# Band attention on folded score tiles: softmax sums and weighted values as 64-row matmuls in two places of a step, and band groups normalized in other steps

## The chip, the cores and the metric

One core of a Trainium2 chip runs the whole program. The metric is device time in microseconds (us). A core has five engines that run their own instruction streams and wait for each other by semaphores: TensorE (PE; its weight loads are shown apart as PEld), VectorE (DVE), ScalarE (ACT), GpSimd (POOL) and SyncE (SP), which issues most DMA transfers. The on-chip memory SBUF has 128 partitions; TensorE writes into PSUM, eight banks of 128 partitions x 512 float32. All data are float32.

## The reference

`x` has the shape (2, 256, 128, 128): two batches, 256 times, 128 bands, 128 channels. One layer:

```
cm = causal_mask(256)             # time j <= time i
bm = band_mask(128, 16)           # |band i - band j| <= 16
x = x + MHA(LN(x), over the 256 times of each band, cm)     # 4 heads of 32
x = x + MHA(LN(x), over the 128 bands of each time, bm)     # 4 heads of 32
x = x + GELU(LN(x) @ w1.T + b1) @ w2.T + b2                 # 128 -> 512 -> 128
MHA: q, k, v = split(x @ wi.T + bi); softmax(q k^T / sqrt(32) + mask) v; @ wo.T + bo
```

## The kernel before

A group is four tiles of 128 tokens (`NT = 4`), 512 columns, and is an object whose methods issue the work of one stage. 128 groups of class `OverTime` come first. Then 16 cycles follow, each of 8 `OverBands` groups (here called k0 to k7; 32 times of one batch, `RUN = 32`) and 8 `FeedForward` groups (f0 to f7) over the same 32 times, whose tokens stay in SBUF as `res` between the two. A cycle takes about 106 us.

`BoundedPath.run` is one loop over n with an order written out by hand. Step n does the scores of group n, the softmax sums and weighted values of n-1 (`weigh`), the output product of n-2, queries, keys and values of n+1, and the layer norm of n+3 (`normalize`, `turn`). The helper `InOrder` passes each instruction on and pins it to program order on its engine, so every operation carries the helper's line, L907 in the profile (L968 in the changed kernel); rows are told apart by tile names.

What a band group does:

- `scores`: for each tile, half of keys and head, a 32x64 matmul `kT` x `qT`. Tokens are bands, so 64 keys see only the 80 queries from 16 below to 16 above: 64 keys by 80 queries. There are four banks `sp`, one for each head; the result lies at its place in a tile of 128 keys x 128 queries, so that a bank has 512 columns, of which 48 in each half tile are not written by these matmuls.
- `first_function`: DVE adds the mask `band` to the scores of the last head (head 3; `by_vector = 1` is the number of such heads), and ACT takes exp of all four heads into `pf` (512 columns each).
- `first_mask`: POOL zeroes what lies outside the band in the other three heads, by two `affine_select` each.
- `weigh`: `sums` of the weights come from matmuls with a matrix of ones (`rp`), the weighted values from `v` (`op`), with all 128 keys on the rows and 32 output rows a head: 4 matmuls of 512 columns, and 16 of 128.
- `invert` (ACT: `ln`, then `r` = exp(-ln)) and `divide` (DVE: one refinement of the reciprocal in `rp`, giving `u`, and `oT` = `op` x `u`), then `output` (`wn`, `oT` into `yp`) and `finish` (DVE: add to x).
- `queries_keys`, `values`: `wf` and `xnT` into `qp`, `kp`, `vp`, which ACT copies out (`qT`, `kT`, `v`).
- `statistics`, `root` (DVE, POOL: `stats`, `mv`, `rstd`), `normalize` (DVE: four `xh`, and a transpose `z` of 32x32 blocks), `turn` and `fetch` (SP: DMAs through DRAM tiles `turned` that finish the transpose as `xnT`).

A feed group does `hidden` (`xnT`, `w1f` into `hp`, two and two banks), GELU by ACT into `hT`, and `weigh` (`w2T_sb`, `hT` into `zp`), which DVE adds to `res`.

The eight PSUM banks go round in order (`turn_of_bank`), two places being held back for `yp` and `qp` of the next groups. float32 matmuls are carried out in two passes: each matmul of the program is two MATMUL and two LDWEIGHTS in the profile. A matmul with 32 output columns of weights uses one of four column strips of the array, and the four strips (in `scores`, eight tiles of 32x64) run beside each other.

Of the kernel before, what the change touches and what calls it, by code (L numbers as in the profile page):

```python
# [33 lines left out]
HALF = P // 2  # L34
LARGE = 1e20
# [334 lines left out]
class Group:  # L370
# [7 lines left out]
    def __init__(self, path, src, dst, before=None, store=None):  # L378
        self.path, self.src, self.dst = path, src, dst
        self.before, self.store = before, store  # L380

# [179 lines left out]
class Attention(Group):  # L561
# [9 lines left out]
    def queries_keys(self):  # L571
        path = self.path
        wf = path.k.wf[self.which]
        self.qp = path.bank([P, NT * P], "qp", self.place.get("qp", path.held.pop("qp", None)))
        product(path, self.qp, wf[:, 0:P], self.xnT)

        self.kp = path.bank([P, NT * P], "kp", self.place.get("kp"))
        product(path, self.kp, wf[:, P : 2 * P], self.xnT)

    def take_query(self):  # L580
        path = self.path
        self.qT = path.work.tile([P, NT * P], F32, name="qT")
        path.scalar.activation(self.qT, self.qp, AF.Identity, bias=path.k.bq[self.which], scale=1.0)

    def take_key(self):
        path = self.path
        self.kT = path.work.tile([P, NT * P], F32, name="kT")
        path.scalar.copy(self.kT, self.kp)

    def values(self):  # L590
        path = self.path
        wv = path.k.wf[self.which][:, 2 * P : 3 * P]
        self.vp = path.bank([P, NT, P], "vp", self.place.get("vp"))
        for i in range(NT):
            product(path, self.vp[:, i], self.xnT[:, i * P : (i + 1) * P], wv, turn=2 if i in self.swapped else 0)

    def take_values(self):
        path = self.path
        self.v = path.work.tile([P, NT, P], F32, name="v", bufs=4)
        path.scalar.copy(self.v, self.vp)  # L600

# [13 lines left out]
    def divide(self):  # L615

        path, vector = self.path, self.path.vector
        if self.r0 is None:
            self.oT = path.work.tile([P, NT * P], F32, name="oT", bufs=2)
            u = path.work.tile([P, NT * P], F32, name="u", bufs=2)  # L620
            vector.tensor_tensor(by_rows(u), by_tile(self.op), by_tile(self.r), ALU.mult)
            vector.tensor_scalar(self.oT, u, -1.0, None, ALU.mult)
            return
# [4 lines left out]
        vector.tensor_tensor(by_rows(self.oT), by_tile(self.op), by_tile(u), ALU.mult)  # L628

    def output(self):  # L630
        path = self.path
        self.yp = path.bank([P, NT, P], "yp", self.place.get("yp", path.held.pop("yp", None)))
        for i in range(NT):
            product(path, self.yp[:, i], self.oT[:, i * P : (i + 1) * P], path.k.wn[self.which])

    def finish(self):
        self.path.vector.tensor_tensor(self.dst(), self.yp, self.dst(), ALU.add)
        if self.store is not None:
            self.store()
# [13 lines left out]
class OverTime(Attention):  # L653
# [7 lines left out]
    def values(self):  # L661
        path = self.path
        wv = path.k.wf[self.which][:, 2 * P : 3 * P]
        self.vp = [path.bank([P, 2, P], "vp", self.place.get(f"vp{s}")) for s in range(2)]
# [5 lines left out]
    def take_values(self):  # L670
        path = self.path
        self.v = path.work.tile([P, NT, P], F32, name="v", bufs=4)
        for s in range(2):
            path.scalar.copy(self.v[:, 2 * s : 2 * s + 2], self.vp[s])

    def first_tiles(self):
# [3 lines left out]
        self.s0 = {h: path.bank([P, 2, 2 * P], "sp", path.banks[f"a{h}"]) for h in range(H)}  # L680

    def second_tiles(self):
# [3 lines left out]
        self.s1 = {h: path.bank([P, 2, P], "sp", path.banks[f"b{h}"]) for h in range(H)}  # L686
# [15 lines left out]
    def first_weights(self, heads):  # L702
        for h in heads:
            self.path.scalar.activation(self.p0[:, :, h], self.s0[h], AF.Exp)

    def second_weights(self, heads):
        for h in heads:
            self.path.scalar.activation(self.p1[:, :, h, 0], self.s1[h], AF.Exp)

# [17 lines left out]
    def weigh(self):  # L727
        path, v = self.path, self.v
        rp = path.bank([P, 2, 2, P], "rp", self.place.get("rp"))
# [4 lines left out]
        op = path.bank([P, 2, 2 * P], "op", self.place.get("op"))  # L734
# [33 lines left out]
class OverBands(Attention):  # L768
# [3 lines left out]
    follow = ("yp",)  # L772
    by_vector = 1

    def scores(self, heads):
        path = self.path
        self.sp = {h: path.bank([P, NT * P], "sp") for h in heads}
        for i in range(NT):
            for e in range(2):
                keys = slice(e * HALF, (e + 1) * HALF)  # L780
                a = i * P + e * (HALF - BAND)
                q = slice(a, a + HALF + BAND)
                for h in heads:
                    r = rows_of(h)
                    path.tensor.matmul(
                        self.sp[h][keys, q], self.kT[r, i * P + e * HALF : i * P + (e + 1) * HALF], self.qT[r, q],
                        start=True, stop=True,
                    )

    def first_function(self):  # L790
        path = self.path
        for h in range(H - self.by_vector, H):
            sp = self.sp[h].rearrange("p (i q) -> p i q", i=NT)
            path.vector.scalar_tensor_tensor(
                sp, sp, LIMIT, path.band.unsqueeze(1).to_broadcast([P, NT, P]), ALU.min, ALU.add
            )
        for h in range(H):
            path.scalar.activation(self.p[:, h].rearrange("p i q -> p (i q)"), self.sp[h], AF.Exp)

    def first_mask(self):  # L800
        path = self.path
        for h in range(H - self.by_vector):
            blk = self.p[:, h]
            for s in (1, -1):
                path.gpsimd.affine_select(
                    out=blk, in_=blk, compare_op=ALU.is_ge, fill=path.zero, base=BAND,
                    pattern=[[0, NT], [-s, P]], channel_multiplier=s,
                )

    def first_half(self):  # L810
        self.p = self.path.work.tile([P, H, NT, P], F32, name="pf", tag="p", bufs=3)
        self.scores(range(H))

    def weigh(self):
        path = self.path

        path.held = {name: path.turn_of_bank() for name in self.follow}
        self.rp = path.bank([P, NT * P], "rp")
        for h in range(H):
            path.tensor.matmul(  # L820
                self.rp[rows_of(h), :], path.k.ones[:, 0:D], self.p[:, h].rearrange("p i q -> p (i q)"),
                start=True, stop=True,
            )
        self.op = path.bank([P, NT * P], "op")
        for i in range(NT):
            c = slice(i * P, (i + 1) * P)
            for h in range(H):
                r = rows_of(h)
                path.tensor.matmul(self.op[r, c], self.v[:, i, r], self.p[:, h, i, :], start=True, stop=True)


class FeedForward(Group):
# [8 lines left out]
    def hidden(self, js):  # L841
        path = self.path
        for j in js:
            self.hp[j] = path.bank([P, NT * P], "hp")
            product(path, self.hp[j], path.k.w1f[:, j * P : (j + 1) * P], self.xnT)

    def gelus(self, js):
        path = self.path
        for j in js:
# [3 lines left out]
            )  # L853

# [14 lines left out]
    def weigh(self):  # L869
        path, NI = self.path, self.path.k.NI  # L870
        if self.last:
            zp = [path.bank([P, P], "zp") for i in range(NT)]
        else:
            self.zp = path.bank([P, NT, P], "zp")
# [11 lines left out]
    def divide(self):  # L886
# [5 lines left out]
        else:  # L892
            self.path.vector.tensor_tensor(self.dst(), self.zp, self.dst(), ALU.add)
        self.store()
# [17 lines left out]
class BoundedPath:  # L912
    def __init__(self, ctx, tc, k):
# [6 lines left out]
        self.next_bank = 0  # L920
        self.inputs = 0
        self.held = {}
# [5 lines left out]
        self.dram = ctx.enter_context(tc.tile_pool(name="turns", bufs=3, space=DRAM))  # L928
# [6 lines left out]
        self.band = once.tile([P, P], F32, name="band")  # L935
        tc.nc.gpsimd.memset(self.band, 0.0)
        for s in (1, -1):
            tc.nc.gpsimd.affine_select(
                out=self.band, in_=self.band, compare_op=ALU.is_ge, fill=-1e30, base=BAND,
                pattern=[[-s, P]], channel_multiplier=s,  # L940
            )

    def turn_of_bank(self):
        i, self.next_bank = self.next_bank, (self.next_bank + 1) % 8
        return i

    def bank(self, shape, name, i=None):

        flat = self.ps[self.turn_of_bank() if i is None else i][:, 0 : math.prod(shape[1:])]
# [4 lines left out]
        return flat.rearrange(f"p ({' '.join(names)}) -> p {' '.join(names)}", **sizes)  # L954

# [218 lines left out]
    def verdict(self):  # L1174

        vector, C = self.vector, P
        tp = self.bank([P, 6], "tp")
# [97 lines left out]
    def run(self, x, out):  # L1275
# [15 lines left out]
        for i in range(len(groups) - 2):  # L1291
            if at(i, OverBands) and at(i + 1, OverBands):
                groups[i].follow = ("yp", "qp")

# [18 lines left out]
        for n in range(len(groups) + 2):  # L1313
# [70 lines left out]
            do_at(n + 3, (OverBands, FeedForward), "normalize", "turn")  # L1384
# [128 lines left out]
```

## Time and profile before

| | |
|---|---|
| three runs | 2632.67, 2633.2, 2638.77 us (median 2633.2) |
| the profiled execution, first to last instruction (its span, the only time shown of it) | 2631.9 us |
| its instructions | 156,460; the granted TensorE clock 1.000 |
| `OverTime` part | about the first 926 us |
| one cycle of band and feed groups | about 106.2 us, 16 times |
| one band step, from scores to scores | 6.23 us |
| one feed step | 6.92 to 6.93 us |
| busy shares | PE 99%, DVE 81%, POOL 74%, ACT 70% |

In the timeline rows a number pair is the start and the length in us; the length of a run of pipelined matmuls reaches past the start of the next, so the start of one row to the start of the next is what it costs TensorE. `[0.30 <-issue]` is idle time ahead of the row and what ended it; `issue` means that the engine waited for nothing that the profile shows. A row of windows gives the stretch, its length, then for PE, PEld, DVE, ACT and POOL the busy time and (x) the instructions, the granted clock, the DMA engines' busy share and GB/s. In the groups the columns are: busy us, mean ns of one | idle us ahead and what ended it.

### The profile page before, as it was taken

The page shows a single profiled execution, that of the slowest core. Times are in us where ns is not written, and L with a number is a line of the kernel's source. Part 1 is how long each engine was busy: PE and PEld are TensorE (multiplying, and loading weights), DVE is VectorE, ACT ScalarE, POOL GpSimd, SP SyncE. Part 2 cuts the span into 40 slices and gives each one's busy share as a digit, 9 for nine tenths or more (in the row PEclk, how much of TensorE's full clock was granted, in tenths as well). Part 3 has the DMA queues.
Part 4 walks back from the last instruction along what each step waited for, and adds up shares of the span by engine and source line. Part 5 has one row for each costly group of instructions (what it writes and reads, how often), then busy time and mean ns, then how long its engine had stood idle before and what let it go on. Part 6 is the DMA issues. An engine that isn't in the chain of part 4 may idle for free.

```text
span 2631.9 us, 156460 instructions
## 1 busy us (share of the span) xinstructions
PE 2617.8 (99%) x68688; PEld 1837.4 (70%) x68688; DVE 2140.8 (81%) x6410; ACT 1838.8 (70%) x3543; POOL 1958.6 (74%) x2311
## 2 busy tenths in 40 slices
PE   9999999999999999999999999999999999999999
PEld 6666666666766767666777776667676677777776
DVE  8888888888888887977878779788797797887974
ACT  7989988999899875564655746647557466475573
POOL 7999999999999987666667666665776666757762
PEclk9999999999999999999999999999999999999999
DMA  6656555565565454445454544554454445554543
GB/s 155 167 149 158 149 149 149 155 155 149 149 158 149 122 127 119 115 123 127 118 124 124 123 122 117 126 128 120 122 126 120 120 119 131 123 120 123 123 104 88
DMA packets 469797, 344.97 MB, mean 131 GB/s; under 512 B 43120, under 2 KB 404464, under 8 KB 469104
## 3 DMA queue, kind: packets, MB, share of 16 engines
q1 hardware_dynamic: 468408, 334.41, 50.5%
q8 instruction: 540, 8.85, 1.5%
q14 instruction: 153, 1.25, 0.2%
q10 hardware_dynamic: 696, 0.46, 0.1%
HBM read 167.98 MB, written 166.72 MB: 127 GB/s over the span
## 4 chain that ended last, share of the span: by engine, by line
PE 99%; DVE 0%; issue 0%; DMA 0%; ACT 0%; ACTq 0%; DVEq 0%
PE bank L907 99%; DMA x<-in_x 0%; DVE xh L907 0%; DVE bank L907 0%; DVE res L907 0%; DVE stats L907 0%; DVE oT L907 0%; DVE u L907 0%; DVE xnT L907 0%; ACTq L907 0%; ACT p L907 0%; DVE vy L907 0%; ACT lnv L907 0%; DVE mv L907 0%; ACT root L907 0%
## 5 line engine op out<-in xcount | busy, mean ns | idle before, releaser
L907 ACT ACTIVATE hT<-bank,b 128x512 f32<-128x512 f32 x512 | 348.1, 688 | 524.2 <-PE bank L907 483.2
L907 POOL TENSOR_SCALAR_AFFINE_SELECT pf<-pf 128x512 f32<-128x512 f32 x768 | 477.7, 637 | 185.3 <-ACT pf L907 159.1
L907 PEld LDWEIGHTS bank<-w2T_sb,hT 128*32 128x32 f32 x16384 | 467.4, 110 | 54.8 <-issue 29.0
L907 PE MATMUL bank<-xnT,wf 128*32 128x512 f32 x4096 | 492.4, 592 | 0.5 <-DVE xnT L907 0.5
L907 PE MATMUL bank<-xnT,w1f 128*32 128x512 f32 x4096 | 486.3, 592 | 0.2 <-issue 0.2
L907 PE MATMUL bank<-w2T_sb,hT 128*32 128x128 f32 x16384 | 482.8, 273 | 1.0 <-issue 1.0
L907 ACT ACTIVATE p<-bank 128x512 f32<-128x512 f32 (+1 forms) x1024 | 430.6, 494 | 62.9 <-PE bank L907 62.9
L907 DVE TENSOR_SCALAR xh<-x,mv,rstd 128x160 f32<-128x160 f32 (+1 forms) x1012 | 394.3, 432 | 59.7 <-POOL rstd L907 49.4
L907 POOL TENSOR_SCALAR_AFFINE_SELECT p<-p 128x1024 f32<-128x1024 f32 (+2 forms) x384 | 364.5, 949 | 57.5 <-ACT p L907 49.1
L907 PEld LDWEIGHTS bank<-wf,xnT 128*32 128x32 f32 x8192 | 243.3, 110 | 144.1 <-issue 101.6
L907 POOL TENSOR_TENSOR p<-p,p 128x512 f32<-128x512 f32 x256 | 324.6, 1291 | 10.6
L907 DVE BATCH_NORM_STATS2 stats<-x 128x6 f32<-128x128 f32 x1536 | 329.0, 276 | 3.4 <-DMA x<-in_x 3.4
L907 POOL TENSOR_SCALAR rstd<-mv 128x4 f32<-128x4 f32 x251 | 57.8, 230 | 361.7 <-DVE mv L907 360.5
L907 PEld LDWEIGHTS bank<-xnT,w1f 128*32 128x32 f32 x4096 | 183.6, 110 | 171.6 <-issue 109.6
L907 PE MATMUL bank<-qT,kT 32*64 32x80 f32 (+4 forms) x16384 | 302.0, 271 | 0.1
L907 PEld LDWEIGHTS bank<-qT,kT 32*64 32x64 f32 x16384 | 260.0, 131 | 51.2 <-ACT kT L907 50.6
L907 DVE TENSOR_TENSOR res<-bank,res 128x512 f32<-128x512 f32 (+1 forms) x259 | 170.3, 658 | 153.3 <-PE bank L907 144.7
L907 ACT ACTIVATE pf<-bank 128x512 f32<-128x512 f32 x512 | 265.8, 602 | 35.5 <-PE bank L907 31.3
L907 PE MATMUL bank<-wn,oT 128*32 128x128 f32 x8192 | 283.8, 274 | 0.1
L907 DVE STREAM_TRANSPOSE z<-xh 128x512 f32<-128x512 f32 x380 | 270.3, 711 | 13.3
L907 PE MATMUL bank<-wf,xnT 128*32 128x128 f32 x8192 | 276.5, 273 | 0.0
L907 POOL TENSOR_TENSOR rstd<-rstd,mhalf 128x4 f32<-128x4 f32 x251 | 260.8, 1039 | 20.9
(100 smaller groups left out, 3820.3 us busy)
## 6 DMA issues: line engine op xcount, KB each, us to landing
turned<-z SPq DMA_DIRECT2D x1520, 64.0 KB, 2.7
xnT<-turned SPq DMA_DIRECT2D x380, 256.0 KB, 3.2
x<-res SPq DMA_DIRECT2D x256, 128.0 KB, 2.5
x<-x SPq DMA_DIRECT2D x128, 256.0 KB, 4.1
out<-res SPq DMA_DIRECT2D x252, 128.0 KB, 2.3
x<-in_x SPq DMA_DIRECT2D x124, 256.0 KB, 4.3
x<-in_x SPq DMA_DIRECT2D x4, 128.0 KB, 2.8
x<-in_x SPq DMA_DIRECT2D x6, 64.0 KB, 2.9
```

The source lines that it names most:

```text
L907: return self.tc.keep_in_program_order(emit(*args, **kwargs))
```

## The change

1. Scores are folded: the bank of a head holds `[P, NT, REACH]` with `REACH = 80`: 64 keys on the lower and 64 on the upper partitions, each with its own 80 queries. Exp, masks and `pf` have 320 columns instead of 512.
2. POOL's six `affine_select` become three multiplications with a 0/1 tile `keep`. DVE's mask is still that of head 3 (`by_vector` is now the head itself), and comes later, just ahead of `weigh(n-1)`; head 3's exp comes after `ln` and `r` of n-1 on ACT.
3. Sums and values are 64-row matmuls of 80 columns, one for each half of keys: 8 program matmuls for the sums and 32 for the values instead of 4 and 16. Both halves add into the same bank over the 32 middle queries. They are issued in two places: `weigh_first(n-1)` (sums of half 1, values of half 0) ahead of the scores of n, where the groups n-1 and n are band groups; and `weigh(n-1)` (sums of half 0, values of half 1) behind them. Its first matmul waits for `seen`, a copy by ACT of one element of what `weigh_first` wrote.
4. The banks are a free list: `give` puts a bank at its end when its reader has been issued, `take` takes the first.
5. In all cycles but the first, band groups are normalized at n-6 where the current step is a band or feed step for which that is due, instead of n-3: in a cycle, the steps k0, k1 do one band group each (the last two of the eight), k2 to k4 none, k5 to k7 the feed groups f0 to f2, and the feed steps f2 to f4 a feed and a band group each. The DRAM pool of `turned` has 8 buffers instead of 3.
6. In the first feed step f0, `output` and `finish` of k6 come between `weigh_first` and `weigh` of k7.

The core of the diff:

```diff
+REACH = HALF + BAND
 class Group:
+    def take(self, name, shape, i=None):
+        free = self.path.free
+        if i is None:
+            i = free[0]
+        if i in free:
+            free.remove(i)
+        self.taken[name] = i
+        return self.path.bank(shape, name, i)
...
 class OverBands(Attention):
-    by_vector = 1
+    by_vector = 3
+    def scores(self):
+        self.sp = {h: self.take(f"sp{h}", [P, NT, REACH]) for h in range(H)}
...
+                keys, a = slice(e * HALF, (e + 1) * HALF), i * P + e * (P - REACH)
+                    path.tensor.matmul(
+                        self.sp[h][keys, i], self.kT[r, i * P + e * HALF : i * P + (e + 1) * HALF],
+                        self.qT[r, a : a + REACH], start=True, stop=True,
+                    )
+    def first_mask(self):
+        keep = path.keep.unsqueeze(1).to_broadcast([P, NT, REACH])
+        for h in range(H):
+            if h != self.by_vector:
+                path.gpsimd.tensor_tensor(self.p[:, h], self.p[:, h], keep, ALU.mult)
...
+    def part(self):
+        seen = path.small.tile([P, 1], F32, name="seen")
+        self.seen = path.scalar.copy(seen, self.op_[:, NT - 1, 0:1])
+    def sums(self, e):
+        rows, a = slice(e * HALF, (e + 1) * HALF), e * (P - REACH)
+        for h in range(H):
+            m = self.path.tensor.matmul(
+                self.rp_[rows_of(h), :, a : a + REACH], self.path.k.ones[rows, 0:D], self.p[rows, h],
+                start=e == 1, stop=True, skip_group_check=True,
+            )
+            if e == 0 and h == 0:
+                self.behind(m)
+    def weighted(self, e):
+        rows, a = slice(e * HALF, (e + 1) * HALF), e * (P - REACH)
+        for i in range(NT):
+            for h in range(H):
+                r = rows_of(h)
+                self.path.tensor.matmul(
+                    self.op_[r, i, a : a + REACH], self.v[rows, i, r], self.p[rows, h, i],
+                    start=e == 0 and i == 0, stop=True, skip_group_check=True,
+                )
+    def weigh_first(self):
+        self.rp_ = self.take("rp", [P, NT, P])
+        self.op_ = self.take("op", [P, NT, P])
...
+        self.sums(1)
+        self.weighted(0)
+        self.part()
+    def weigh(self):
+        self.sums(0)
+        self.weighted(1)
...
-        self.dram = ctx.enter_context(tc.tile_pool(name="turns", bufs=3, space=DRAM))
+        self.dram = ctx.enter_context(tc.tile_pool(name="turns", bufs=2 * NT, space=DRAM))
...
 def run(self, x, out):
+        def turn_ahead(n):
+            for i in (n + 3, n + 6):
+                if at(i, FeedForward) and i == n + 3 or at(i, OverBands) and (i == n + 3 or n > run0[0] and i not in run0):
+                    if not hasattr(groups[i], "turned"):
+                        do(i, "normalize", "turn")
...
+            if bands[1] and bands[2]:
+                do(n - 1, "weigh_first")
             do(n, "first_half", "first_function", "first_mask")
...
-            do_at(n + 3, (OverBands, FeedForward), "normalize", "turn")
+            turn_ahead(n)
...
+            do_at(n, OverBands, "late_mask")
+            if turn:
+                do(n - 1, "weigh_first")
+                do(n - 2, "output", "finish")
             do(n - 1, "weigh")
             do(n - 1, "invert_exactly" if turn else "invert")
+            do_at(n, OverBands, "late_function")
...
-            if bands[2] or turn:
+            if bands[2]:
                 do(n - 2, "output", "finish")
```

How the order moves is shown in the seventh run of band groups, from the last two scores of group k3 on. In a row the first name is what is written, the others what is read, and the size is that of one result; `bank_108` to `bank_115` are the eight PSUM banks, `xN` at the end counts alike rows.

On TensorE before, from the end of one step's scores to the next step's:

```order
L907 MATMUL bank_114<-qT,kT 64x80
L907 MATMUL bank_115<-qT,kT 64x80
L907 MATMUL bank_110<-pf,ones 32x512 x4
L907 MATMUL bank_111<-pf,v 32x128 x16
L907 MATMUL bank_108<-wn_241,oT 32x128 x16
L907 MATMUL bank_109<-xnT,wf_238 32x512 x4
L907 MATMUL bank_112<-xnT,wf_238 32x512 x4
L907 MATMUL bank_113<-wf_238,xnT 32x128 x16
L907 MATMUL bank_114<-qT,kT 64x80
L907 MATMUL bank_115<-qT,kT 64x80
```

On TensorE after, the same stretch:

```order
L968 MATMUL bank_112<-qT,kT 64x80
L968 MATMUL bank_110<-qT,kT 64x80
L968 MATMUL bank_114<-pf,ones 32x4x80 x4
L968 MATMUL bank_113<-pf,v 32x80 x16
L968 MATMUL bank_108<-wn_253,oT 32x128 x16
L968 MATMUL bank_115<-xnT,wf_250 32x512 x4
L968 MATMUL bank_109<-xnT,wf_250 32x512 x4
L968 MATMUL bank_111<-wf_250,xnT 32x128 x16
L968 MATMUL bank_112<-pf,ones 32x4x80 x4
L968 MATMUL bank_110<-pf,v 32x80 x16
L968 MATMUL bank_108<-qT,kT 64x80
L968 MATMUL bank_114<-qT,kT 64x80
```

The sums and values of 512 and 128 columns have become 4 and 16 of 80 columns behind the scores, and as many again, of the next group, ahead of the next scores. Those scores take banks 114 and 113, which hold the sums and weighted values of the group before.

On ACT before, the same step:

```order
L907 ACTIVATE pf<-bank_112 128x512
L907 ACTIVATE pf<-bank_113 128x512
L907 ACTIVATE pf<-bank_114 128x512
L907 ACTIVATE pf<-bank_115 128x512
L907 ACTIVATE ln<-bank_110 128x512
L907 ACTIVATE r_33769<-ln 128x512
L907 ACTIVATE qT<-bank_109,bq_283 128x512
L907 COPY kT<-bank_112 128x512
L907 COPY v<-bank_113 128x512
```

On ACT after:

```order
L968 COPY seen<-bank_113 128x1
L968 ACTIVATE pf<-bank_109 128x320
L968 ACTIVATE pf<-bank_111 128x320
L968 ACTIVATE pf<-bank_112 128x320
L968 ACTIVATE ln<-bank_114 128x512
L968 ACTIVATE r_34758<-ln 128x512
L968 ACTIVATE pf<-bank_110 128x320
L968 ACTIVATE qT<-bank_115,bq_295 128x512
L968 COPY kT<-bank_109 128x512
L968 COPY v<-bank_111 128x512
```

Three exps stand ahead of `ln` instead of four, and the fourth behind `r`; the copy `seen` stands ahead of all.

On DVE before, the same step:

```order
L907 SCALAR_TENSOR_TENSOR bank_115<-bank_115,band 128x512
L907 TENSOR_SCALAR xh<-x_58,mv,rstd 128x5x32 x4
L907 STREAM_TRANSPOSE z<-xh 128x512
L907 TENSOR_TENSOR x_31475<-bank_108,x_31475 128x512
L907 TENSOR_TENSOR bank_110<-bank_110,r_33769 128x512
L907 SCALAR_TENSOR_TENSOR u<-bank_110,r_33769 128x512
L907 TENSOR_TENSOR oT<-bank_111,u 128x4x4x32
L907 BN_STATS stats<-x_31475 128x6 x4
L907 BN_AGGR mv<-stats 128x2 x4
```

On DVE after:

```order
L968 SCALAR_TENSOR_TENSOR bank_110<-bank_110,band 128x320
L968 TENSOR_TENSOR x_32316<-bank_108,x_32316 128x512
L968 TENSOR_TENSOR bank_114<-bank_114,r_34758 128x512
L968 SCALAR_TENSOR_TENSOR u<-bank_114,r_34758 128x512
L968 TENSOR_TENSOR oT<-bank_113,u 128x4x4x32
L968 BN_STATS stats<-x_32316 128x6 x4
L968 BN_AGGR mv<-stats 128x2 x4
```

`xh` and `z` are gone from this step; the release of banks 114 and 113 is the third to fifth row.

More of the change, by code (lines that the diff above doesn't have):

```diff
@@ L663, in values @@
         wv = path.k.wf[self.which][:, 2 * P : 3 * P]
-        self.vp = [path.bank([P, 2, P], "vp", self.place.get(f"vp{s}")) for s in range(2)]
+        self.vp = [self.take(f"vp{s}", [P, 2, P], self.place.get(f"vp{s}")) for s in range(2)]
         for i in range(NT):
@@ L679, in first_tiles @@
         self.p0 = path.work.tile([P, 2, H, 2 * P], F32, name="p0", tag="p", bufs=3)
-        self.s0 = {h: path.bank([P, 2, 2 * P], "sp", path.banks[f"a{h}"]) for h in range(H)}
+        self.s0 = {h: self.take(f"s0{h}", [P, 2, 2 * P], path.banks[f"a{h}"]) for h in range(H)}
     def second_tiles(self):
@@ L685, in second_tiles @@
         self.p1 = path.work.tile([P, 2, H, 2, P], F32, name="p1", tag="h", bufs=2)
-        self.s1 = {h: path.bank([P, 2, P], "sp", path.banks[f"b{h}"]) for h in range(H)}
+        self.s1 = {h: self.take(f"s1{h}", [P, 2, P], path.banks[f"b{h}"]) for h in range(H)}
     def first_scores(self, h, s, e):
@@ L800, in first_mask @@
     def first_mask(self):
         path = self.path
[L802 to L812, printed above, removed]
@@ new lines, in late_function, with behind @@
+    def late_function(self):
+        self.weights(self.by_vector)
+    def part(self):
+        path = self.path
+        seen = path.small.tile([P, 1], F32, name="seen")
+        self.seen = path.scalar.copy(seen, self.op_[:, NT - 1, 0:1])
+    def behind(self, matmul):
+        self.path.tc.add_manual_dep(
+            matmul.ins, self.seen.ins.name,
+            mybir.DependencyInfo(mybir.DependencyClass.Sync, mybir.DependencyReason.DATA),
+            reason="row tiles take turns in a bank",
+        )
```

108 lines of the change are left out of this document (56 added, 52 removed).

## The prediction

> **What bounds the kernel now.** I read the page's totals and the chain that ended last first, then TensorE's timeline over a band step, then the places where TensorE stands still.
>
> ```profile
> span 2631.9 us, 156460 instructions
> PE 2617.8 (99%) x68688; PEld 1837.4 (70%) x68688; DVE 2140.8 (81%) x6410; ACT 1838.8 (70%) x3543; POOL 1958.6 (74%) x2311
> PE 99%; DVE 0%; issue 0%; DMA 0%; ACT 0%; ACTq 0%; DVEq 0%
> q8 instruction: 540, 8.85, 1.5%
> ```
>
> TensorE is the bound: 99% of the chain. The last line is a queue that loads instructions: 540 packets of 8.85 MB, 16 KB each. TensorE executes 68,688 matmuls and as many weight loads, 137,376 in all, or 254 to a packet, so this is its code. One band step:
>
> ```profile
> 1603.52 0.40 PE L907 MATMUL bank<-wf,xnT 128*32 128x128 f32 x8
> 1603.85 0.97 PE L907 MATMUL bank<-qT,kT 32*64 32x80 f32 x64
> 1604.74 1.07 PE L907 MATMUL bank<-pf,ones 128*32 128x512 f32 x8
> 1605.63 1.06 PE L907 MATMUL bank<-pf,v 128*32 128x128 f32 x32
> 1606.50 1.06 PE L907 MATMUL bank<-wn,oT 128*32 128x128 f32 x32
> 1607.37 1.90 PE L907 MATMUL bank<-xnT,wf 128*32 128x512 f32 x16
> 1609.09 1.06 PE L907 MATMUL bank<-wf,xnT 128*32 128x128 f32 x32
> 1610.08 0.97 PE L907 MATMUL bank<-qT,kT 32*64 32x80 f32 x64
> ```
>
> From start to start: scores 0.89 (0.90 below), sums 0.89, values 0.87, output 0.87, queries and keys 1.72, v 0.99; 6.23 us in all, with no idle time. Each matmul has a weight load, so a step is 184 + 184 = 368 instructions. Where does TensorE stop?
>
> ```profile
> 1568.70 1.74 PE L907 MATMUL bank<-w2T_sb,hT 128*32 128x128 f32 x56 [0.20 <-issue]
> 1599.81 0.64 PE L907 MATMUL bank<-pf,v 128*32 128x128 f32 x16 [0.30 <-issue]
> 1568.69:1599.80 31.11, 30.81 (x896) 19.90 (x896) 25.77 (x61) 24.35 (x45) 20.09 (x34) 1.00 0.46 115
> 1565.49:1568.69 3.20, 3.02 (x138) 2.65 (x136) 2.06 (x5) 3.11 (x5) 0.56 (x1) 1.00 0.13 44
> 1778.13:1780.81 2.68, 2.68 (x134) 2.58 (x131) 1.54 (x4) 2.52 (x4) 0.00 (x0) 1.00 0.02 6
> 1353.45:1357.01 3.56, 3.14 (x144) 2.78 (x142) 2.48 (x6) 3.53 (x6) 0.94 (x2) 1.00 0.02 5
> 1357.01 0.75 PE L907 MATMUL bank<-w2T_sb,hT 128*32 128x128 f32 x20 [0.42 <-issue]
> ```
>
> The two stops of this cycle wait for nothing that the profile shows, in the middle of runs of like matmuls, and between them lie 896 + 896 = 1792 = 7 x 256 instructions: they fall on the ends of 16 KB packets. The three short windows are single packets of 256 (the counts include what was in flight at the ends): 3.20 and 3.56 us are packets that ended in a stop, 2.68 one that did not. So I read the stops as a packet that ran out before the next had landed, the next being asked for only when this one starts. A packet must then last at least a time L, seen here at 2.68 or less to 3.56; before, hardly any stretch of 256 instructions is shorter than that.
>
> **The change, part by part.**
>
> *Sums and values.* The two pieces cost 0.89 + 0.87 = 1.76 us. Each becomes halves of 80 columns: a slot (sums of one half beside values of the other) has 8 + 32 matmuls and 40 loads, 80 instructions. The sums' row gives the column rate: 2 passes of 512 in 0.89 us. In a slot each of eight tiles gets 2 x 4 x 80 = 640 columns, 0.56 us; the scores, also 640 columns in each of eight tiles with as many loads as the values have here, take 0.90. Ends 0.56 and 0.90; I take 0.72 between them, because the slot issues 80 instructions to the scores' 128 but has the same eight loads in half its tiles. A step is now scores 0.90, slot 0.72, output 0.87, queries and keys 1.72, v 0.99, slot 0.72: 5.92 instead of 6.23, with 128 + 80 + 64 + 32 + 64 + 80 = 448 instructions. In a run of eight groups: 8 x (1.76 - 1.44) = 2.56 us less. In f0 the output stands between the two slots: two more changes of tile shape, each about the 0.99 - 0.87 by which v outlasts the output product of the same size, 0.1 as an estimate. Net -2.36 us a run.
>
> *Code.* 448 instructions in 5.92 us are 256 in 3.38 on average, but unevenly. Cutting four steps (1792) into seven packets from the start of the scores, with each piece's instructions spread evenly, gives 2.27, 4.10, 4.01, 2.36, 4.44, 2.06 and 4.44 us. If long packets give nothing to short ones, the stops are the sum of what each lacks to L. At 3.20: 0.93 + 0.84 + 1.14 = 2.91 for four steps, 0.73 a step, and for the seven steps of a run with both slots 5.1 us. At 2.68 it is 1.35, 0.34 a step, 2.4 a run; at 3.56 it is 3.99, 1.0 a step, 7.0 a run. I take 3.20, the middle row. Five normalizes' DMAs leave the band steps and the window of 3.20 has DMA share 0.13, those of 2.68 and 3.56 both 0.02, so DMA load doesn't order them. The old stops, 0.20 + 0.30 in this cycle, are within the new ones: -0.5.
>
> [...]
>
> *Banks.* The next scores of heads 1 and 2 now write the banks of sums and values of the group before, so they wait for its divide. The pieces of that loop:
>
> ```profile
> 1572.96 0.97 PE L907 MATMUL bank<-qT,kT 32*64 32x80 f32 x64
> 1573.97 2.07 ACT L907 ACTIVATE pf<-bank 128x512 f32<-128x512 f32 x4 [0.29 <-PE bank L907]
> 1575.90 0.63 ACT L907 ACTIVATE ln<-bank 128x512 f32<-128x512 f32 x1
> 1576.56 0.63 ACT L907 ACTIVATE r<-ln 128x512 f32<-128x512 f32 x1
> 1577.22 0.70 DVE L907 TENSOR_TENSOR bank<-bank,r 128x512 f32<-128x512 f32 x1 [0.15 <-ACT r L907]
> 1577.96 0.69 DVE L907 SCALAR_TENSOR_TENSOR u<-bank,r 128x512 f32<-128x512 f32 x1
> 1578.75 0.69 DVE L907 TENSOR_TENSOR oT<-bank,u 128x512 f32<-128x512 f32 x1
> 1574.72 1.60 DVE L907 TENSOR_SCALAR xh<-x,mv,rstd 128x160 f32<-128x160 f32 x4
> 1576.36 0.71 DVE L907 STREAM_TRANSPOSE z<-xh 128x512 f32<-128x512 f32 x1
> 1591.21 0.86 DVE L907 BATCH_NORM_STATS2 stats<-x 128x6 f32<-128x128 f32 x4
> 1591.99 0.36 DVE L907 BATCH_NORM_AGGREGATE mv<-stats 128x2 f32<-128x6 f32 x4
> L907 ACT ACTIVATE p<-bank 128x512 f32<-128x512 f32 x512 | 292.2, 597 | 0.6 <-PE bank L907 0.6
> L907 ACT ACTIVATE p<-bank 128x256 f32<-128x256 f32 x512 | 183.6, 390 | 62.3 <-PE bank L907 62.3
> L907 POOL TENSOR_SCALAR_AFFINE_SELECT pf<-pf 128x512 f32<-128x512 f32 x768 | 477.7, 637 | 185.3 <-ACT pf L907 159.1
> L907 POOL TENSOR_TENSOR p<-p,p 128x512 f32<-128x512 f32 x256 | 324.6, 1291 | 10.6
> ```
>
> With scores at t, exp begins at t + 1.01. An exp of 512 columns takes 1.93 / 4 = 0.48 of ACT, and 192 columns fewer save 192 x (597 - 390) / 256 = 155 ns: 0.33 each. Three end at t + 2.0, `ln` and `r` take 0.66 each, the divide 0.74 + 0.79 + 0.69: t + 5.5, against the next scores at t + 5.92. That hides in k2 to k4. In k5 and k6 DVE also normalizes a feed group (1.60 + 0.71) and takes statistics (1.2), and k1's step lacks a slot: some 0.5, 0.2 and 0.5, at most 1.2 a run. A stop for code ahead of the scores gives that time back; I count 0.4 (ends 0 and 1.2).
>
> *Masks and exps.* POOL's three multiplications at 1291 x 320/512 = 0.81 us each replace six selects of 0.64: 2.4 for 3.8. Beginning at t + 1.3, and with a group's `rstd` between, they end by t + 4.6, ahead of their reader at t + 5.20. Head 3's exp behind `r` ends at t + 3.7. The copy `seen` is one element, behind which three exps queue; it is issued at the end of the first slot, a whole score stretch (0.90) ahead of its reader. All cost nothing under that cover; if POOL were late, the first slot would be, by the same amount in each step.
>
> *Normalizing.* The moved work was off TensorE's path before (DVE is 81% busy). Where it goes:
>
> ```profile
> 1634.63:1641.55 6.92, 6.92 (x164) 4.53 (x160) 6.85 (x32) 2.75 (x5) 6.63 (x9) 1.00 0.43 100
> 1655.41:1662.33 6.92, 6.92 (x164) 4.53 (x160) 3.91 (x15) 2.75 (x5) 4.16 (x5) 1.00 0.41 92
> ```
>
> An early feed step already fills DVE for 6.85 of 6.92 us. With two normalizes (2 x 2.3), two sets of statistics (2 x 1.2) and the addition to `res` (about 0.7) f2 to f4 need 7.6, so DVE falls 0.7 a step behind, about 2 us, and the later steps (3.91 busy) make it up. What stands behind it is the addition out of `zp`, whose bank is not taken again for over 2 us, and the tiles of groups that are fetched steps later. SP's queue gets five DMAs for each group moved (four of `turned`, one `xnT`), behind the same `z`, where DMA is 0.41 to 0.43 busy. Cost 0; without that cover up to 2 us a run, +32.
>
> *Sum.* -2.36 + 5.1 + 0.4 - 0.5 = +2.64 us a run; 16 runs give +42, so 2674 for the profiled execution. Its span of 2631.9 is 1.3 below the median 2633.2, so 2675 on the scale of the runs. The unknowns: L from 2.68 to 3.56 gives -43 to +30; a slot of 0.90 adds 0.36 a step, half of which comes out of stops, about +20, and 0.56 the reverse, about -18.
>
> **The rivals.**
>
> *Faster: no stops for code.* If the loader runs several packets ahead, the mean of 3.38 us is above 3.20 and no packet is late; then -2.36 - 0.5 + 1.2 (the bank waits, now uncovered) = -1.66 a run, -27: 2607. For it: the saving on TensorE is certain arithmetic if slots overlap. Against it: packets of TensorE that are shorter than the others do stop before, although their neighbours are long. It decides where L falls below 2.1 or the lookahead is two packets. 0.23.
>
> *No change: L near 2.7.* Stops of 2.4: -2.36 + 2.4 + 0.4 - 0.5 = 0 a run, 2633. The 2.68 row, a packet that didn't stop, speaks for it. 0.12.
>
> *Halves in turn.* If tiles on rows 0 to 63 and 64 to 127 wait for one another, a slot is 0.56 + 0.56 and a switch, about 1.2: 8 x (1.76 - 2.4) = +5.1 a run instead of -2.56; the steps then are 6.9 us and lack little for code (some 0.1 a step): about +6 a run, 2730. The scores' 640 columns in 0.90, eight tiles in the time of one and a half, speak against it. 0.05.
>
> *Banks hold every step.* If the late mask, the addition of `finish` and the divide together reach t + 6.4 in all seven steps, it costs 7 x 0.48 = 3.4 and covers the stops: +0.5 a run, 2642. 0.05.
>
> **How the numbers follow.** Stops for code that outweigh the saving have 0.55, with a range of their own of 2642 to 2705. Under 0.3% (8 us) is what a measurement of this kernel can't tell from no change. Faster is the first rival, 0.23; same 0.12; slower 0.55 + 0.05 + 0.05 = 0.65. The range of 2605 to 2708 leaves out half of the first rival, the third and the tail of the forecast, some 0.2.
>
> **What would show it.** PE's instructions rise by 10,240 to 147,616, and the loader's packets to about 580. In band steps TensorE has stops "issue" of 0.8 to 1.2 us, some three in four steps, 256 instructions apart or a multiple; pieces otherwise last as above, slots 0.72, steps 6.6 to 6.7. Stops ahead of the scores that end with DVE (`oT`) are the bank loop; ahead of a slot with POOL (`pf`), late masks. Slots above 1.1 mean halves in turn. The forecast is wrong if no stops show and steps are 5.9 to 6.0.

## The result and the profile after

The changed kernel takes 2792.1 us (2786.5 to 2798.8) against 2633.4 for the kernel before: a ratio of 1.060, 95% interval 1.0585 to 1.0618. Slower, as forecast, but by 159 us where 42 were, and outside the range. The page of the profiled execution:

```profile
span 2794.4 us, 166813 instructions
PE 2708.5 (97%) x73808; PEld 1835.5 (66%) x73808; DVE 2123.4 (76%) x6410; ACT 1778.6 (64%) x3671; POOL 1807.2 (65%) x1934
q8 instruction: 581, 9.52, 1.5%
PE 88%; DVE 6%; issue 3%; DMA 1%; SPq 1%; POOL 0%; ACT 0%; DVEq 0%; ACTq 0%; POOLq 0%
```

TensorE executes 2 x 73,808 = 147,616 instructions and its loader fetches 581 packets, as counted beforehand. It is 97% busy instead of 99%, and the chain now also passes through DVE, through `issue` (waits for nothing that the profile shows) and through DMAs. One band step that has no stop, in TensorE's timeline (start and length in us):

```profile
1650.73 0.97 PE L968 MATMUL bank<-qT,kT 32*64 32x80 f32 x64
1651.63 0.47 PE L968 MATMUL bank<-pf,ones 64*32 64x320 f32 x4
1651.65 0.48 PE L968 MATMUL bank<-pf,v 64*32 64x80 f32 x16
1651.92 0.45 PE L968 MATMUL bank<-pf,ones 64*32 64x320 f32 x4
1651.95 0.78 PE L968 MATMUL bank<-pf,v 64*32 64x80 f32 x16
1652.67 1.08 PE L968 MATMUL bank<-wn,oT 128*32 128x128 f32 x32
1653.57 1.90 PE L968 MATMUL bank<-xnT,wf 128*32 128x512 f32 x16
1655.28 1.06 PE L968 MATMUL bank<-wf,xnT 128*32 128x128 f32 x32
1656.27 0.47 PE L968 MATMUL bank<-pf,ones 64*32 64x320 f32 x4
...
1657.31 0.32 PE L968 MATMUL bank<-qT,kT 32*64 32x80 f32 x8
```

The step is 6.58 us (1650.73 to 1657.31) where I had 5.92 and before had 6.23. Scores, output, queries and keys, and v last what they did; the slots last 1.04 each (1651.63 to 1652.67), not 0.72. Sums and values do start beside each other, 0.02 us apart; but of the last 16 value matmuls (1651.95), which begin 0.30 us after the first 16, the row is 0.78 long and not 0.48. Single instructions show where: in at least 226 of the 256 slots one gap of 0.20 us lies between the first and the second pass of tile 3's first value matmul, and the few matmuls behind it come further apart than those ahead.

What TensorE waits for (engine and tile <- what ended the wait: us in all, times, longest):

```profile
PE bank L968 <- issue: 56.6, 68, 2.3
PE bank L968 <- DMA xnT<-turned: 6.1, 7, 1.4
...
PE bank L968 <- DVE res L968: 3.2, 2, 2.1
PE bank L968 <- DVE mv L968: 2.5, 3, 0.9
```

These count only time in which no modelled matmul is running. So I also took, from starts of instructions, the gaps of more than 0.12 us beyond the columns of the matmul ahead. Most of these are the gaps in the slots; of the others, 81 fall on one position: with TensorE's instructions numbered, they stand at 193 modulo 256 (two more or less), the same position as in the kernel before, and make 72.8 us; before it was 12 and 5.0 us. I call these stops at packet ends. By place, scores of k0 to scores of k7 take 840.0 us in the 16 runs (708.3 before), the feed groups with what surrounds them 1029.2 (997.6).

One thing that the profile of before never showed, in TensorE's timeline and then in a window (length, busy PE, PEld, DVE, ACT, POOL, granted clock, DMA share, GB/s):

```profile
1761.68 0.43 PE L968 MATMUL bank<-wn,oT 128*32 128x128 f32 x2 [1.99 <-issue]
```

```profile
1761.68:1765.10 3.42, 3.42 (x22) 1.68 (x26) 2.60 (x4) 0.69 (x1) 0.00 (x0) 0.51 0.02 5
```

A stop of 1.99 us is followed by 3.42 us at a granted clock of 0.51. Not every such stop is; this longer one of the same execution was not:

```profile
2233.30 0.52 PE L968 MATMUL bank<-wn,oT 128*32 128x128 f32 x9 [2.14 <-issue]
```

```profile
2233.30:2236.70 3.40, 3.40 (x85) 2.35 (x89) 2.71 (x5) 1.54 (x3) 0.00 (x0) 1.00 0.02 5
```

Over the span the clock is 0.994, so the slow stretches cost 0.006 x 2794 = 17 us at most.

### The profile page after: what moved, and what is told of

Read it like the earlier page. It is cut to its first block, busy times and chain, and to the rows that moved or that the text cites. A ratio compares the mean times of both kernels' runs of the same rounds, so it can differ in the third digit from the quotient of the medians.

```text
span 2794.4 us, 166813 instructions
## 1 busy us (share of the span) xinstructions
PE 2708.5 (97%) x73808; PEld 1835.5 (66%) x73808; DVE 2123.4 (76%) x6410; ACT 1778.6 (64%) x3671; POOL 1807.2 (65%) x1934
## 4 chain that ended last, share of the span: by engine, by line
PE 88%; DVE 6%; issue 3%; DMA 1%; SPq 1%; POOL 0%; ACT 0%; DVEq 0%; ACTq 0%; POOLq 0%
PE bank L968 88%; DVE xh L968 2%; DVE stats L968 1%; DMA xnT<-turned 1%; SPq L968 1%; DVE z L968 1%; DVE res L968 1%; DVE mv L968 1%; DVE ln L968 0%; POOL rstd L968 0%; DVE x L968 0%; DVE u L968 0%; DVE oT L968 0%; DMA x<-x 0%; DMA x<-in_x 0%
## 5 line engine op out<-in xcount | busy, mean ns | idle before, releaser
L968 POOL TENSOR_TENSOR pf<-pf,keep 128x320 f32<-128x320 f32 x384 | 323.6, 873 | 359.4 <-ACT pf L968 359.3
L968 PE MATMUL bank<-xnT,wf 128*32 128x512 f32 x4096 | 506.2, 600 | 6.1 <-issue 5.5
L968 PEld LDWEIGHTS bank<-w2T_sb,hT 128*32 128x32 f32 x16384 | 454.5, 110 | 72.1 <-issue 57.0
L968 PE MATMUL bank<-xnT,w1f 128*32 128x512 f32 x4096 | 480.5, 595 | 16.8 <-DMA xnT<-turned 6.1
L968 PE MATMUL bank<-w2T_sb,hT 128*32 128x128 f32 x16384 | 475.9, 273 | 1.9 <-issue 1.8
L968 PEld LDWEIGHTS bank<-wf,xnT 128*32 128x32 f32 x8192 | 249.0, 110 | 147.4 <-issue 102.8
L968 PEld LDWEIGHTS bank<-xnT,w1f 128*32 128x32 f32 x4096 | 134.7, 110 | 232.8 <-issue 164.3
L968 PE MATMUL bank<-wf,xnT 128*32 128x128 f32 x8192 | 284.3, 273 | 1.1 <-issue 1.0
L968 PE MATMUL bank<-pf,v 64*32 64x80 f32 x8192 | 267.9, 235 | 15.1 <-issue 13.3
```

Source lines behind the costliest of these rows:

```text
L968: return self.tc.keep_in_program_order(emit(*args, **kwargs))
```

## Experiments

The theory after the result: (A) the loss is the slots' 1.04 us, the stops at packet ends, and feed steps in which the moved normalizes come too late. "Step" is the shortest of k2 to k7, "stops" those at packet ends, counted as above. Each ratio is to the kernel before as it ran beside that run (medians from 2633 to 2639 us).

| run | median us | ratio to before | TensorE instructions in a band step | step us | stops: times, us |
|---|---|---|---|---|---|
| before | 2633 | | 368 | 6.23 | 12, 5 |
| after | 2792 | 1.0602 | 448 | 6.58 | 81, 73 |
| normalizes back | 2773 | 1.0507 | 448 | 6.58 | 82, 74 |
| tile 0 ahead of the sums | 2787 | 1.0576 | 448 | 6.06 | 108, 109 |
| both | 2745 | 1.0410 | 448 | 6.06 | 98, 105 |
| half the value code | 2635 | 1.0010 | 384 | 5.91 | 30, 16 |
| before, normalizes moved | 2656 | 1.0070 | 368 | 6.23 | 11, 5 |
| the same, behind the addition | 2672 | 1.0141 | 368 | 6.23 | 20, 11 |
| before, sums in 128 columns | 2666 | 1.0117 | 416 | 6.24 | 44, 23 |
| before, queries and keys too | 2805 | 1.0634 | 512 | 6.49 | 213, 151 |
| the same, normalizes moved | 2830 | 1.0733 | 512 | 6.94 | 211, 152 |

**Does code bound it? The kernel before with more instructions.**

```diff
-        for h in range(H):
-            path.tensor.matmul(self.rp[rows_of(h), :], path.k.ones[:, 0:D], self.p[:, h]...)
+        for i in range(NT):
+            for h in range(H):
+                path.tensor.matmul(self.rp[rows_of(h), i * P : (i + 1) * P], path.k.ones[:, 0:D], self.p[:, h, i], ...)
...
+            product(path, self.qp[:, c], wf[:, 0:P], self.xnT[:, c])   # c: 128 columns, for i in range(NT); kp too
```

> The kernel before, with the band groups' sums, queries and keys as matmuls of 128 columns instead of 512: the same columns and the same results, 512 TensorE instructions in a band step instead of 368, and nothing else. Theory A, a packet of 256 instructions must last as long as the next one takes to land (in the trace of before the next one lands, and is taken up, a median of 3.6 us after a packet begins): 512 in 6.23 us are two packets of about 2.7 and 3.6 us, so a step stops for some 1.2 us, 8 steps by 16 runs: about 2780 (2740 to 2840), stops 256 instructions apart. Rival B, TensorE's code is fetched far enough ahead and the stops of the changed kernel have another cause: 2633, at most 10 us more for the loads.

2804.6 us, 1.063 (1.0605 to 1.0663): instructions alone, with no column added, cost as much as the whole change, and 146 us of it (151 less 5) are stops at packet ends. Its timeline:

```profile
2333.22 0.66 PE L921 MATMUL bank<-qT,kT 32*64 32x80 f32 x35
2334.48 0.53 PE L921 MATMUL bank<-qT,kT 32*64 32x80 f32 x29 [0.60 <-issue]
2334.93 1.08 PE L921 MATMUL bank<-pf,ones 128*32 128x128 f32 x32
2335.83 1.06 PE L921 MATMUL bank<-pf,v 128*32 128x128 f32 x32
2336.71 1.25 PE L921 MATMUL bank<-xnT,wf 128*32 128x128 f32 x35
2338.50 0.96 PE L921 MATMUL bank<-xnT,wf 128*32 128x128 f32 x27 [0.54 <-issue]
```

Between the two stops lie 29 + 32 + 32 + 35 = 128 matmuls and as many loads: one packet of 256, 4.02 us long where its matmuls need 3.48. Rival B is out. The smaller dose had the sums alone in 128 columns:

> The dose to the dense run: the kernel before with the sums alone as matmuls of 128 columns, 416 TensorE instructions in a band step, the columns unchanged. Packets of 256 then last 2.66, 4.25, 4.58, 2.78, 4.67, 2.87, 4.05 us and so on; with about 3.75 us from a packet's start until the next can be used, the five short ones of a run lack about 1 us each: 4.5 to 5 us a run, 70 in all, against 5 before. Theory A: 2705 (2690 to 2725), some 5 stops a run. Rival B, the cost goes by the number of instructions added: 48 of 144, a third of the dense run's 166 us: 2690 or less. Rival C, no packets: 2636.

2665.8 us, 1.0117 (1.0093 to 1.0141). The sign and the kind are right, the size is not: 44 stops of 0.5 us, not 80 of 1 us. Rival B's "2690 or less" covers it, and the cost isn't in proportion either, since 48 of 144 instructions would give 55 us and it is 31. A fixed time for each packet, as I used it, is too simple. In the trace the stops do follow the landing: at these 44 and at those of the dense run TensorE goes on about 1.4 us (median) after the loader's packet has landed. What varies most is when the loader begins: in the middle eight tenths of the 44, 0.6 to 2.4 us after TensorE began the packet ahead. What decides that stays open.

**Do other DMAs set the time of a packet?** The run with 512 instructions, with normalizes moved out of the band steps:

> The dense run (512 instructions in a band step) with the band groups normalized at n-6 as in the changed kernel, which takes the DMAs of five of eight normalizes out of the band steps. Tells whether other DMA traffic sets the time in which a code packet lands. Theory A, it doesn't (the changed kernel with and without the moved normalizes had the same stops, 73 and 74 us): the dense run's stops of 151 us stay, the feed steps cost 20: 2825 (2812 to 2835). Rival B, fewer DMAs let packets land sooner: stops below 120 us and 2790 or less.

2830.1 us, stops 152 us against 151. Theory A held, but the dose was smaller than I wrote, here and in the prediction: k0 and k1 keep a band normalize each and k5 to k7 their feed normalizes, so three of eight leave the band steps, not five. The traces show it: between scores of k0 and the first `w1f` matmul of the feed groups stand 128 transposes `z` in the 16 runs of the dense kernel, and 83 here. Taking the transfers of three of eight normalizes away left the stops as they were; a stronger test was not made.

**The moved normalizes.** Undone in the changed kernel, then done alone in the kernel before:

```diff
-            turn_ahead(n)
+            do_at(n + 3, (OverBands, FeedForward), "normalize", "turn")
```

> The changed kernel with one part undone: every band group is normalized at n-3 again (DRAM pool still 8). Theory A, from the two traces: the loss is slots of 1.04 us (about +50 us), 81 stops at the ends of code packets (73 us against 5 before) and some 20 us of feed steps that wait for xnT. Only the last belongs to this part: 2792 becomes about 2770 (2755 to 2785), no waits for xnT ahead of w1f, code stops and slots as before. Rival B, the moved normalizes are most of the loss (DVE too late in f2 to f4): below 2720. Rival C, DVE's normalizes now stand ahead of the divide and the next scores wait for the banks of sums and values: above 2800.

2773.0 us, ratio 1.0507 (1.0488 to 1.0527): 19 us come back, as theory A had it, and the stops stay. In the profiled executions the feed part is 14 us shorter (1029.2 to 1015.4), the band part 12 (840.0 to 827.7, at a clock of 0.996 instead of 0.994), and the part ahead of them 4 longer. Rival B is out, and C too.

> The kernel before with one part of the change alone: band groups normalized at n-6 by the changed kernel's rule, and 8 DRAM tiles. Theory A: f2 to f4 wait for xnT as in the changed kernel, about 1 us a run: 2650 (2640 to 2665). Rival B, the work hides and costs nothing: 2633. Rival C, moving it out of the band steps is a gain there (code packets land sooner with fewer DMAs): 2628.

2655.7 us, 1.0070 (1.0050 to 1.0089): +17 by its own runs; in the profile the loss lies in the feed part (1020.3 against 997.6). The time is as theory A had it, but TensorE waits more for DVE's addition than for `xnT` (7.1 and 4.5 us). How it costs, in the timelines of TensorE and DVE there:

```profile
1863.83 1.90 PE L907 MATMUL bank<-xnT,w1f 128*32 128x512 f32 x16
1866.09 1.92 PE L907 MATMUL bank<-xnT,w1f 128*32 128x512 f32 x16 [0.36 <-DVE res L907]
...
1865.37 0.66 DVE L907 TENSOR_TENSOR res<-bank,res 128x512 f32<-128x512 f32 x1
```

TensorE stops in the middle of `w1f`, and goes on 0.06 us after DVE's addition out of `zp` has ended (1865.37 + 0.66 = 1866.03). Then I put the band group's normalize behind that addition:

```diff
+                far = i == n + 6                       # in turn_ahead(n, late)
+                    if far == late and not hasattr(groups[i], "turned"):
...
             do(n - 1, "divide")
+            turn_ahead(n, True)
```

> The kernel before with the moved normalizes (as in the run of that part alone, 2656), but in f2 to f4 the band group's normalize stands on DVE behind the addition out of zp instead of ahead of it. Theory A: TensorE waits there in the middle of w1f because DVE, 0.7 us a step behind, gives the bank of zp back late; with the addition ahead of 2.3 us of work most of that goes: 2642 (2636 to 2648). Rival B, xnT of the later feed groups is what is late, and the order within a step changes nothing: 2656.

2672.3 us, 1.0141 (1.0124 to 1.0158): worse, and both theories missed. TensorE's waits in the run ahead and in this one:

```profile
PE bank L907 <- DVE res L907: 7.1, 16, 2.1
PE bank L907 <- DMA xnT<-turned: 4.5, 6, 1.0
```

```profile
PE bank L907 <- DMA xnT<-turned: 11.1, 17, 1.4
PE bank L907 <- ACT kT L907: 7.8, 14, 0.6
```

The waits for the addition are gone, as A said, but those for `xnT` are more than twice as long and new ones for `kT` stand in band steps. The edit did more than I wrote ahead of it: the band normalizes of f5 to f7 and those of the last two band groups in k0 and k1 moved behind as well, so the waits for `kT`, all of them in k3, may come from there; that was not taken apart. What is shown is that the lateness moves and does not go.

**The gap in a slot.** The first pass of the first sum has 320 columns, its second pass as many; behind that come 12 instructions of sums and 64 of values. In both slots of a step I put four value matmuls (16 instructions) ahead of the sums; the first slot's edit:

```diff
-        self.sums(1)
-        self.weighted(0)
+        self.weighted(0, range(1))       # tile 0
+        self.sums(1)
+        self.weighted(0, range(1, NT))
```

> The changed kernel with another order in a slot and the same instructions: values of tile 0 first, then the sums, then the values of tiles 1 to 3. In the changed kernel every slot stands still for 0.20 us at the values of tile 3, some 62 instructions behind the second pass of the first sum, and goes on when that pass has ended. Theory A, TensorE gets only so many instructions (about 64) ahead of the oldest one that has not ended: now at most 60 follow, the stall goes, slots are about 0.84 us, 256 x 0.20 = 52 us less, of which code stops give back about half: 2765 (2740 to 2775). Rival B, the stall belongs to tile 3 or to a bank or rows that two tiles share: slots stay 1.04 and the time 2792.

No slot has the gap of 0.20 us, and the timeline of one without a stop is:

```profile
2460.86 0.27 PE L970 MATMUL bank<-pf,v 64*32 64x80 f32 x4
2460.89 0.47 PE L970 MATMUL bank<-pf,ones 64*32 64x320 f32 x4
2460.95 0.45 PE L970 MATMUL bank<-pf,v 64*32 64x80 f32 x15
2461.18 0.43 PE L970 MATMUL bank<-pf,ones 64*32 64x320 f32 x1
2461.18 0.23 PE L970 MATMUL bank<-pf,v 64*32 64x80 f32 x1
2461.19 0.44 PE L970 MATMUL bank<-pf,ones 64*32 64x320 f32 x3
2461.23 0.39 PE L970 MATMUL bank<-pf,v 64*32 64x80 f32 x12
2461.56 1.16 PE L970 MATMUL bank<-wn,oT 128*32 128x128 f32 x31
```

0.70 us (2460.86 to 2461.56), shorter than the 0.84 I expected: the gap cost a slot 0.34, not only its own 0.20. The step is 6.06, 0.52 shorter. By the slots theory A is right and rival B out. But the kernel takes 2786.7 us (ratio 1.0545 to 1.0607), 5 less and outside the 2740 to 2775 forecast: stops rise from 73 to 109 us, and more than I expected is given back. With the normalizes back as well:

> The changed kernel with both repairs: values of tile 0 ahead of the sums in a slot, and band groups normalized at n-3 again. Theory A: the feed steps' waits go (about 20 us), the slot's 0.26 us go but come back as stops for code; 2792 less 20 less 5 is 2767 (2755 to 2775), with over 100 us of stops at packet ends, and every other wait near none: the code alone keeps it above the kernel before. Rival B, the two repairs help each other: below 2740.

2744.6 us, 1.0410 (1.0392 to 1.0427): some 23 better than the sum of the two, so below theory A's range, and not below 2740 as rival B had it; stops 105 us. The repair of the slot is worth 28 us where the feed groups don't wait, and 5 where they do. Whether they interact is open: the runs of the slot repair alone spread most (2776 to 2800), and in the profiled executions the repair is worth 20 us (2794.4 to 2774.5) and 27 (2772.6 to 2745.3), nearly the same.

**Take the code away.** If code and the gap are what is left, fewer value instructions must bring nearly everything back:

```diff
-        for i in range(NT):
+        for i in range(0, NT, 2):
...
-                    self.op_[r, i, a : a + REACH], self.v[rows, i, r], self.p[rows, h, i],
+                    self.op_[r, i : i + 2, a : a + REACH], self.v[rows, i, r], self.p[rows, h, i : i + 2],
```

> The run with the band groups normalized at n-3 again (2773), and each pair of value matmuls of neighbouring tiles replaced by one of 160 columns with the first tile's values: the second tile's values are left out, the columns stay. 384 TensorE instructions in a band step instead of 448; sums first in a slot, as in the changed kernel. Theory A, what is left of the loss is code and the stall in the slot: only 44 instructions now follow the first sum, so slots lose the 0.20 us although sums stand first; packets last 3.4, 3.5 and 5.2 us, so code stops fall from 74 us to under 15; steps 6.06; 2640 (2628 to 2655). Rival B, banks, masks or the copy ahead of the second slot hold the steps: above 2690. Rival C, sums first is itself what stalls a slot: slots 1.04 and steps 6.6, about 2690.

2634.8 us, 1.0010 (1.0001 to 1.0020): 138 us of the 140 that remained over before are gone. Slots shorter by 0.34 are 256 x 0.34 = 87 us, and stops fall by 58: together a little more than that. A step there:

```profile
2432.34 0.97 PE L968 MATMUL bank<-qT,kT 32*64 32x80 f32 x64
2433.24 0.47 PE L968 MATMUL bank<-pf,ones 64*32 64x320 f32 x4
2433.27 0.48 PE L968 MATMUL bank<-pf,v 64*32 64x160 f32 x8
2433.53 0.45 PE L968 MATMUL bank<-pf,ones 64*32 64x320 f32 x4
2433.56 0.45 PE L968 MATMUL bank<-pf,v 64*32 64x160 f32 x8
2433.95 1.08 PE L968 MATMUL bank<-wn,oT 128*32 128x128 f32 x32
2434.84 1.90 PE L968 MATMUL bank<-xnT,wf 128*32 128x512 f32 x16
2436.56 1.06 PE L968 MATMUL bank<-wf,xnT 128*32 128x128 f32 x32
2437.55 0.47 PE L968 MATMUL bank<-pf,ones 64*32 64x320 f32 x4
...
2438.25 0.97 PE L968 MATMUL bank<-qT,kT 32*64 32x80 f32 x64
```

Slots of 0.71 with the sums first, so their order as such is no cause (rival C out); the step is 5.91. Banks, masks and the copy `seen` stay as in the changed kernel and hold little (rival B out): TensorE waits 14 times for `oT`, 2.8 us in all. Yet it isn't faster than before: 30 stops, 16 us in all, are still there, against 12 and 5 us, and take back a part of what shorter steps save. The rest was not placed.

## Why the prediction was wrong

- **Slots: the step that failed.** I bounded a slot by 0.56 and 0.90 and took 0.72; it is 1.04. The bound of 0.90 came from the scores, whose matmuls are all equally short. It left out that a slot begins with matmuls of 320 columns and can stand still behind them: the gap of 0.20 us comes at about the 64th instruction behind the second pass of the first sum, and there is none where only 60 follow (tile 0 ahead) or 44 (half the code). Without it a slot is 0.70 or 0.71, beside the 0.72 that I had chosen between two ends. 16 x (1.04 - 0.72) = 5.1 us a run, 82 in all. That the shortest step of 6.58 lies beside the 6.6 to 6.7 I named as a sign is luck: that step has no stop and two slots of 1.04.
- **Code: right in kind, and nearly in size by two errors.** Forecast 5.1 us a run of stops; measured 72.8 / 16 = 4.5. With steps of 6.58, my 3.20 us to a packet would have given 3.1: packets 2.59, 4.42, 4.33, 2.68, 4.83, 2.56 and 4.83 us lack 1.77 in four steps. So 3.20 was too short; the packet above was 4.02. That the next packet is asked for only when one starts was my reading of the windows; at the dense run's stops the loader began it a median of 1.2 us after TensorE had begun the one ahead. The run with both repairs shows this term by itself: with slots of 0.70 its stops are 105 us, 6.6 a run. The rival without stops is out: with the sums in 128 columns 256 instructions have 6.23 x 256/416 = 3.83 us on average, more than 3.20, and there are 44 stops, so long packets don't pay for all that short ones lack.
- **Normalizing: failed.** I costed it at nothing because the banks of `zp` come back in time, and gave 32 us as the price without that cover; it cost 17 to 19. The longest wait for the addition out of `zp`, 2.1 us, fits the backlog of 2 us; the cover was wrong. That five normalizes leave the band steps was a misreading, it is three; the sum doesn't use it.
- **Banks, masks, exps:** no wait of TensorE ends with `oT` in the changed kernel's list of waits, so the 0.4 us a run weren't there. With half the value code, where steps are as short as predicted, such waits appear, 2.8 / 16 = 0.2 a run.
- **Clock:** not foreseen, up to 17 us.
- **Sum:** 42 forecast; + 82 (slots) + 19 (normalizes) - 5 (stops: 68 more than before, 73 forecast) - 6 (banks) + up to 17 (clock) is up to 149 of the 159 measured. At least 10 us stay unplaced, and the terms don't simply add: without the slots' gap and the moved normalizes the kernel still takes 110 us more than before, in part because stops rise to 105. "Halves in turn", the rival nearest to the time, had the wrong mechanism: the halves overlap.

## What to carry to other kernels

Where TensorE is busy 99%, count instructions as well as columns: cutting matmuls into shorter pieces saves little if each piece still brings its two loads (here two slots took 1.40 us at best for 1.76), and stretches of 256 instructions shorter than the time to the next packet can stop though the mean is long enough (44 stops at a mean of 3.83 us, with the sums in 128 columns). How many instructions of short matmuls stand behind a long one is worth a run: here 76 behind the second pass of a sum of 320 columns brought a gap of 0.20 us in a slot, 60 or 44 brought none. And shortening such a step pays only once its code is short too: here 0.52 us of 6.58 came back as 5 to 28 us of a possible 67.

## What the runs showed of the hardware

- From a stop at a packet's end to the next one, 256 instructions took 4.02 us in the dense run where the matmuls need 3.48; by the trace of all queues at its stops the loader's packet itself took 0.9 to 1.5 us, was begun a median of 1.2 us after TensorE began the packet ahead of it, and TensorE went on 1.2 to 1.5 us after it had landed. All stops at packet ends together were 5 us in the kernel before and 151 in the dense run.
- At about the 64th instruction behind the second pass of a sum of 320 columns a slot stood still for 0.20 us; where only 60 or 44 instructions follow that pass, it didn't. That their number is the cause is inferred from these three kernels; what sets the number was not shown.
- After an idle time of 1.99 us the granted clock was 0.51 for 3.42 us. It isn't the length alone: after 2.14 us of idle time in the same execution the clock stayed 1.00.
- Matmuls of the four heads run beside each other in their column strips: the four of the sums' first pass in the first slot above start within 0.02 us of each other at 1651.63, and the four of the second pass 0.29 us later.
